# One product moved behind the silu switch, and rows of B spread at unit ends, in the Mamba layer of a four-layer stack

## The chip, the cores and the metric

The kernel runs on one core of one Trainium2 chip. The metric is device time of one launch in microseconds. All names of engines are those of the profile: PE is TensorE, PEld its weight loads, DVE is VectorE, ACT is ScalarE, POOL is GpSimd, SP is the queue that issues DMAs.

## The reference

Four layers work on an image tensor x of 8 images, 192 channels and 56 by 56 positions, each as `x = x + layer(group_norm(x))`. Layer 0 is an involution. Layers 1, 2 and 3 are selective scans (Mamba blocks); layer 1 runs the block three times for each image, on 64 channels each, with an inner width of 512. Cut to what matters here:

```python
xz = x @ in_proj_W.T                       # xi, z
xc = silu(causal_conv4(xi) + conv_b)
dbl = xc @ x_proj_W.T                      # dt_rank | B (16 states) | C (16 states)
dt = softplus(dbl[..., :DT_RANK] @ dt_proj_W.T + dt_proj_b)
h  = h * exp(dt * A) + (dt * xc) * B       # for each position, channel and state
y  = sum_over_states(h * C) + xc * D
y  = y * silu(z)
out = y @ out_proj_W.T
```

## The kernel before

Positions are cut into chunks of 448 (8 rows of the image), 7 chunks to an image, 56 in all. A job is one chunk through one block: layer 1 has 168 jobs (three a chunk, called kinds 0, 1 and 2 here, after the index i in `mamba_jobs`), layers 2 and 3 have 56 each. A job is cut into units: nd groups of 128 channels times NQ = 4 quarters of the states. Layer 1 has nd = 4, so 16 units a job, m = 0 to 15, and 2688 units; layers 2 and 3 have nd = 3, so 12 units a job. One unit holds 4 rows (r) of 448 positions on 128 partitions, where a partition is a channel and a state.

The order of all instructions is written out by hand in `ssm_layer`, unit by unit, and each engine works through its own stream in that order. For unit k the steps are:

- `decays(k, h)` (L749), ACT: exp(dt * A) into the PSUM tiles da0 and da1, two rows for each half h.
- `inputs_begin(k)` (L757), ACT: the carried state goes into column 0 of the tile uhg (nine buffers); issued three units ahead.
- The product (dt * xc) * B into uhg, for half of the units by POOL (`inputs_by_pool`, L768, B from rows in SBUF that SP loads, issued two units ahead), for the others by DVE (`inputs_by_vector`, L774, issued one unit ahead, B from PSUM).
- `spread_b(k)` (L743), PE: for a unit of DVE, one bf16 matmul that spreads the row of B to all 128 partitions, into a pool of one PSUM bank. So the next one can't be written before the product that reads the last one is done.
- `scan(k, 0)` and `scan(k, 1)` (L778), DVE: the recurrence, two scans of 898 positions.
- `keep(k)` (L782), ACT: the last state goes to the carry.
- `readout(k)` (L787), POOL: h * C in place, issued two units late. `reduce(k)`, PE: the sum over the states (L796), with the D term ahead of it for the first quarter of a group (L793), issued three units late.
- `gated(g)` (L812), DVE: times silu(z), at the start of the unit with q = 3. `nothing` (L802): matmuls with a zero weight, as filler on PE.

Beside this the next job is prepared, in steps with costs that `places` deals out over the 32 places of a job (two a unit: before `scan(k, 0)` and before `scan(k, 1)`): convolution (L1046), silu, x_proj (L621), the left-over parts of B (L632, L633), the deltas (L655), softplus (L663), dt times x (L667 on PE, L670 on DVE), the gate (L1064). Two of them are blocks that change ACT's table of functions and change it back. The first is the silu switch: silu of the next job's xc (L616) and of this job's z (L597), ended by a table load (L589). It lies at place 6, so in unit m = 3 of layer 1; the last job's `out_proj` (L1074, L1076, ten matmul passes on PE) follows at place 7 of the same unit. The second is softplus, in unit 7 where the job is of kind 0 and in unit 9 where it is of kind 1 or 2.

In layer 1 POOL has the products of units 1, 3, 5, 7, 9, 11, 13 and 15 before the change, and SP loads rows of B for the quarters 1 and 3. The stream of a unit reads, cut to what the change touches:

```python
scan(k, 0); decays(k + 1, 0); inputs_begin(k + 3)
inputs_by_pool(k + 2); readout(k - 2)
inputs_by_vector(k + 1)
spread_b(k + 2)
bg.run(plan[2 * m + 1]); nothing(k - 3, more > 1)
load_when_free(k)
scan(k, 1); keep(k); decays(k + 1, 1)
```

Of the kernel before, what the change touches and what calls it, by code (L numbers as in the profile page):

```python
# [86 lines left out]
def conv_mamba_stack(ctx: ExitStack, tc: tile.TileContext, a, out):  # L87
# [503 lines left out]
    def with_gates(ops, u):  # L591


        def all_ops():
            ops()
            if u is not None:
                nc.scalar.activation(u.zs, u.zs, AF.Silu)  # L597

        table_block(all_ops)
# [112 lines left out]
    def ssm_layer(pool, w, jobs, n_slots):  # L712


        nd = w.nd
        units = [(i, j, q) for i in range(len(jobs)) for j in range(nd) for q in range(NQ)]
        groups = [(i, j) for i in range(len(jobs)) for j in range(nd)]
        per_job = nd * NQ
        pool_units = {1, 3, 5, 7, 9, 11, 13, 15} if nd == 4 else {1, 3, 6, 7, 9, 11}
        pool_rows = sorted({m % NQ for m in pool_units})  # L720
        us = [Layer() for _ in jobs]
        carry = []
        for s in range(n_slots):
# [1 line left out]
        reps, brow, uhg, ys = {}, {}, {}, {}  # L725

        def load_ops(g):

            i, j = groups[g]
            reps[g] = t = pool.tile([128, NR, 2, T], F32, tag="rep", name="rep", bufs=2)  # L730
            for r in range(NR):
                src = us[i].ops[j][32 * r : 32 * r + 32].rearrange("e c t -> e (c t)")
                nc.sync.dma_start(
                    out=t[:, r].rearrange("p c t -> p (c t)"), in_=src.unsqueeze(1).to_broadcast([32, 4, 2 * T])
                )

        def spread_b(k):

            if k in by_pool:
                return  # L740
            i, j, q = units[k]
            brow[k] = banks.b.tile([128, 512], F32, tag="b", name="b")
            nc.tensor.matmul(brow[k][:, :T], lhsT=pick_b[:, q, :], rhs=us[i].parts, start=True, stop=True)  # L743

        def decays(k, h):
            i, j, q = units[k]
            t = banks.da[h]
            for r in range(2):
                nc.scalar.activation(  # L749
                    t[:, 64 + 449 * r : 512 + 449 * r], reps[k // NQ][:, 2 * h + r, 0, :], AF.Exp, scale=w.neg_a[:, j * NR + 2 * h + r, q : q + 1]  # L750
                )

        def inputs_begin(k):
            i, j, q = units[k]
            uhg[k] = pool.tile([128, NR, T + 1], F32, tag="uhg", name="uhg", bufs=9)
            before = zeros[:, :NR] if jobs[i][1] else carry[jobs[i][0]][:, j, q, :]
            nc.scalar.copy(uhg[k][:, :, 0:1], before.unsqueeze(2))  # L757

        by_pool = {k for k in range(len(units)) if (k % per_job) in pool_units}

        def inputs_by_pool(k):
            if k not in by_pool:
                return
            i, j, q = units[k]
            b = us[i].rows[0, q].unsqueeze(1).to_broadcast([128, NR, T])
            nc.gpsimd.tensor_mul(uhg[k][:, :, 1:], reps[k // NQ][:, :, 1, :], b)  # L768

        def inputs_by_vector(k):  # L770
            if k in by_pool:
                return
            b = brow[k][:, :T].unsqueeze(1).to_broadcast([128, NR, T])
            nc.vector.tensor_mul(uhg[k][:, :, 1:], reps[k // NQ][:, :, 1, :], b)  # L774

        def scan(k, h):
            v = uhg[k][:, 2 * h : 2 * h + 2, :].rearrange("p r t -> p (r t)")
            nc.vector.tensor_tensor_scan(v, banks.da[h][:, 63:961], v, 0.0, ALU.mult, ALU.add)  # L778

        def keep(k):  # L780
            i, j, q = units[k]
            nc.scalar.copy(carry[jobs[i][0]][:, j, q, :].unsqueeze(2), uhg[k][:, :, T:])  # L782
# [6 lines left out]
        def reduce(k):  # L789
            i, j, q = units[k]  # L790
            if q == 0:
                ys[k // NQ] = banks.y.tile([128, 512], F32, tag="y", name="y")
                nc.tensor.matmul(ys[k // NQ][:, :T], lhsT=w.dd[:, j, :], rhs=us[i].xc[:, j, :], start=True, stop=False)  # L793
            y = ys[k // NQ]
            for r in range(NR):
                nc.tensor.matmul(y[32 * r : 32 * r + 32, :T], lhsT=fold, rhs=uhg[k][:, r, 1:], start=False, stop=(q == NQ - 1))  # L796

        def nothing(k, n):

            if k >= 0 and units[k][2] < NQ - 1:  # L800
                for _ in range(n):
                    nc.tensor.matmul(  # L802
                        ys[k // NQ][:, : nd * 112], lhsT=zeros, rhs=w.dd.rearrange("p j e -> p (j e)")[:, : nd * 112],
                        start=False, stop=False,
                    )

        def load_of(steps):
            return sum(st.cost for st in steps if st.matmuls)

        def gated(g):  # L810
            i, j = groups[g]
            nc.vector.tensor_mul(us[i].zs[:, j, :], us[i].zs[:, j, :], ys[g][:, :T])  # L812

        n_places = 2 * per_job
        def bounds(job):

            silu = 8 if nd == 3 else 6
            softplus = silu + (6 if nd == 3 else 8 if job[0] == 1 else 12)
            return (0, silu), (silu, silu + 2), (silu + 2, softplus), (softplus, softplus + 1), (softplus + 2, softplus + 4), (softplus + 4, n_places)

        def places(*stretches):

            plan = [[] for _ in range(n_places)]
            for steps, first, end in stretches:
                todo, debt = list(steps), 0.0
                for p in range(first, end):
                    room, closed = (sum(st.cost for st in todo) + debt) / (end - p) - debt, False
                    while todo and (room > 1e-6 and not closed or p == end - 1):  # L830
                        if (todo[0].block if p % 2 else todo[0].settles) and p < end - 1:
                            break
                        plan[p].append(todo[0])
                        closed = todo[0].closes
                        room -= todo.pop(0).cost
                    debt = max(0.0, -room)
            return plan
# [21 lines left out]
        n_units = len(units)  # L859

        def load_when_free(k):

            g = len(reps)
            if g < len(groups) and k >= NQ * g - NQ - 1 and groups[g][1] in us[groups[g][0]].ops:
                load_ops(g)

        for k, (i, j, q) in enumerate(units):
            m = k % per_job
            if m == 0:

                fetch, outs, rest = tail
                if i + 1 < len(jobs):
                    u = us[i + 1]
                    at = bounds(jobs[i + 1])
                    stretches = *jobs[i + 1][2](u, us[i], outs), rest + jobs[i + 1][3](u)
                    plan = places(*((steps, *p) for steps, p in zip(stretches, at)))
                else:
                    gates = Step(None, lambda: with_gates(lambda: None, us[i]), 0, 0.3, block=True)
                    plan = places(([gates], 4, 6), (outs + rest, 8, n_places))
                plan[3][:0] = [Step(None, fetch, 2, 0.0)]  # L880

            if i + 1 < len(jobs) and m - (per_job - NQ) in pool_rows:
                us[i + 1].row_in(0, m - (per_job - NQ))
            if i and m < NQ:
                us[i].row_in(1, m)
            if k >= NQ + 3 and q == 3:
                gated(k // NQ - 1)
            if k >= 3:
                reduce(k - 3)

            more = 3 - math.ceil(load_of(plan[2 * m] + plan[2 * m + 1]))
            nothing(k - 3, more > 2)
            bg.run(plan[2 * m])
            nothing(k - 3, more > 0)
            load_when_free(k)
            scan(k, 0)
            if k + 1 < n_units:
                decays(k + 1, 0)
            if k + 3 < n_units:
                inputs_begin(k + 3)  # L900
            if k + 2 < n_units:
                inputs_by_pool(k + 2)
            if k >= 2:
                readout(k - 2)
            if k + 1 < n_units:
                inputs_by_vector(k + 1)
            if k + 2 < n_units:
                spread_b(k + 2)
            bg.run(plan[2 * m + 1])
            nothing(k - 3, more > 1)  # L910
            load_when_free(k)
            scan(k, 1)
            keep(k)
            if k + 1 < n_units:
                decays(k + 1, 1)
            if m == per_job - 1:
                tail = jobs[i][4](us[i])
# [333 lines left out]
```

## Time and profile before

| | |
|---|---|
| time, median of 3 runs | 24955.37 us (24948.31 to 24965.5) |
| the profiled execution: time, span | 24963.74 us, 24961.9 us |
| mean granted PE clock | 0.817 |
| layer 1, from its first scan to the first of layer 2 | 1607.75 to 17125.96 us, 15518.21 us |
| layer 2, layer 3 | 3976.24 us, 3859.70 us |
| DVE busy | 22616.8 us (91%) |
| POOL busy | 23597.2 us (95%) |
| PE busy, ACT busy | 21153.9 us (85%), 17043.4 us (68%) |

Time and span are of one execution; the median is of three others. Busy is a share of the span. A row of the groups of instructions gives the line, the engine and the operation, output and inputs by name, shapes and count, then the busy time in us and the mean of one in ns, then the idle time of the engine just before them and what ended it. A row of the timeline gives the start and the length in us, and in square brackets the idle time ahead of it.

### The profile page before, as it was taken

The numbers are of one execution on the slowest core, as the hardware profiler recorded it, in microseconds if no ns is written. First come the engines' busy times: TensorE is split into PE (matmuls) and PEld (weight loads), VectorE is DVE, ScalarE is ACT, GpSimd is POOL, SyncE is SP. The second block draws the span as 40 slices with busy tenths as digits, with TensorE's granted clock in tenths as the row PEclk, the third lists the DMA queues.
The fourth block names the chain that finished last, engine by engine and source line by source line (L and its number), as shares of the span: only waits on it lengthen the run. The fifth ranks groups of instructions, "written<-read, shape, count | busy, mean of one in ns | idle before, by whom it ended". The sixth has DMA issues, their size and how long they took to land.

```text
span 24961.9 us, 237862 instructions
## 1 busy us (share of the span) xinstructions
PE 21153.9 (85%) x74220; PEld 6587.3 (26%) x74220; DVE 22616.8 (91%) x15661; ACT 17043.4 (68%) x32578; POOL 23597.2 (95%) x6996
## 2 busy tenths in 40 slices
PE   8988888888888888888888888888888888888888
PEld 2222222222222222222222222222333332333332
DVE  8989999999999999999999999997999998999998
ACT  2247777777767777777777777776777776777776
POOL 6679999999999999999999999998999998999999
PEclk9987777777777777777777777778888888888888
DMA  4433333333333333333333333333444443444443
GB/s 110 110 108 123 121 123 123 121 121 124 124 122 121 123 123 123 122 123 122 121 125 123 121 122 122 125 122 112 140 132 139 139 138 121 140 141 143 142 141 127
DMA packets 1184899, 3132.97 MB, mean 126 GB/s; under 512 B 163756, under 2 KB 446404, under 8 KB 1183496
## 3 DMA queue, kind: packets, MB, share of 16 engines
q1 hardware_dynamic: 1180824, 3116.70, 38.2%
q8 instruction: 582, 9.54, 0.2%
q14 instruction: 693, 5.68, 0.1%
q10 hardware_dynamic: 2800, 1.06, 0.0%
HBM read 2399.92 MB, written 555.55 MB: 118 GB/s over the span
## 4 chain that ended last, share of the span: by engine, by line
DVE 35%; PE 24%; ACT 17%; issue 11%; POOL 7%; DMA 4%; SPq 1%; DVEq 0%; POOLq 0%; ACTq 0%
DVE uhg L778 24%; ACT da L749 8%; DVE uhg L774 7%; PE y L796 4%; POOL uhg L787 4%; PE mm L655 4%; DMA rows<-bc 2%; PE y L802 2%; POOL uhg L768 2%; ACT L589 2%; PE y L793 2%; PE mm L632 2%; DMA rep<-ops 2%; ACT zs L597 1%; PE mm L429 1%
## 5 line engine op out<-in xcount | busy, mean ns | idle before, releaser
L778 DVE TENSOR_TENSOR_SCAN uhg<-da,uhg 128x898 f32<-128x898 f32 x8064 | 15905.1, 2009 | 1279.9 <-ACT da L749 1276.6
L787 POOL TENSOR_TENSOR uhg<-uhg,rows 128x1792 f32<-128x1792 f32 x4032 | 14739.8, 3676 | 275.4 <-ACT carry L782 267.4
L749 ACT ACTIVATE da<-rep,k 128x448 f32<-128x448 f32 x16128 | 10254.0, 636 | 1669.3 <-DVE uhg L778 1291.5
L768 POOL TENSOR_TENSOR uhg<-rep,rows 128x1792 f32<-128x1792 f32 x2016 | 8038.6, 3987 | 481.6 <-DMA rows<-bc 212.7
L796 PE MATMUL y<-uhg,k 128*32 128x448 f32 x32256 | 4780.6, 669 | 757.6 <-POOL uhg L787 755.3
L774 DVE TENSOR_TENSOR uhg<-rep,b 128x1792 f32<-128x1792 f32 x2016 | 4025.5, 1997 | 468.8 <-PE b L743 424.1
L782 ACT COPY carry<-uhg 128x4 f32<-128x4 f32 x4032 | 787.3, 195 | 3547.9 <-DVE uhg L778 3464.2
L793 PE MATMUL y<-xc,w_d 128*128 128x448 f32 x2016 | 1485.7, 832 | 1390.0 <-DVE zs L812 1388.3
L802 PE MATMUL y<-w_d,k 128*128 128x448 f32 (+1 forms) x5276 | 2496.8, 581 | 0.0
L796 PEld LDWEIGHTS y<-uhg,k 128*32 128x32 f32 x32256 | 695.9, 117 | 3858.8 <-issue 2203.8
L655 PE MATMUL mm<-dbl,w_dt 36*128 36x448 f32 (+1 forms) x2016 | 1501.2, 858 | 155.0 <-ACT k L637 155.0
L1102 PE MATMUL mm<-v,w_in 96*128 96x448 f32 x2688 | 1464.8, 677 | 170.1 <-ACT zs L694 71.1
L802 PEld LDWEIGHTS y<-w_d,k 128*128 128x128 f32 x5276 | 1050.9, 214 | 1480.4 <-issue 1452.5
L1046 PE MATMUL mm<-xs,k 128*128 128x448 f32 x2688 | 1229.7, 592 | 112.4 <-ACT zs L694 100.5
L1129 PE MATMUL mm<-xin,w_conv 128*128 128x448 f32 x2688 | 1077.9, 543 | 1.0 <-ACT xin L696 0.9
L441 DVE TENSOR_TENSOR prod<-mm,shifted 128x448 f32<-128x448 f32 x1680 | 928.6, 611 | 141.2 <-PE mm L429 63.5
L632 PE MATMUL mm<-dbl,k 16*16 16x448 f32 x1120 | 687.8, 702 | 422.7 <-ACT dbl L625 422.7
L667 PE MATMUL mm<-xc,k 128*128 128x448 f32 x2016 | 971.4, 592 | 30.8 <-DVE dt L670 29.7
L793 PEld LDWEIGHTS y<-xc,w_d 128*128 128x128 f32 x2016 | 443.3, 258 | 2056.5 <-DVE zs L812 1392.8
L1064 PE MATMUL mm<-xs,k 64*128 64x448 f32 x1344 | 861.6, 750 | 109.0 <-ACT zs L694 109.0
L743 PE MATMUL b<-k,k 96*128 96x448 bf16 x2016 | 832.2, 413 | 126.8 <-DVE uhg L774 126.6
L449 POOL TENSOR_TENSOR x<-x,one 96x448 f32<-96x448 f32 x560 | 631.1, 1134 | 265.9 <-DVE one L441 248.4
(138 smaller groups left out, 19672.2 us busy)
## 6 DMA issues: line engine op xcount, KB each, us to landing
rep<-ops SPq DMA_DIRECT2D x4032, 448.0 KB, 5.9
ops<-dt SPq DMA_DIRECT2D x1008, 448.0 KB, 3.3
rows<-bc SPq DMA_DIRECT2D x1792, 224.0 KB, 6.2
shifted<-xpad SPq DMA_DIRECT2D x672, 179.0 KB, 4.5
xg<-stream SPq DMA_DIRECT2D x168, 336.0 KB, 3.8
xr<-stream SPq DMA_DIRECT2D x168, 336.0 KB, 5.3
stream<-xr SPq DMA_DIRECT2D x112, 336.0 KB, 3.4
xs<-xg SPq DMA_DIRECT2D x224, 112.0 KB, 2.3
```

The costliest lines, as they stand in the source:

```text
L632: nc.tensor.matmul(u.left[m][:NS, :T], lhsT=ident[:NS, :NS], rhs=u.dbl[:NS, :], start=True, stop=False)
L655: nc.tensor.matmul(u.dps[j][:, :T], lhsT=w.dtw[:, j * 128 : (j + 1) * 128], rhs=u.dbl[:nk, :], start=True, stop=True)
L749: nc.scalar.activation(t[:, 64 + 449 * r : 512 + 449 * r], reps[k // NQ][:, 2 * h + r, 0, :], AF.Exp, scale=w.neg_a[:, j * NR + 2 * h + r, ...
L768: nc.gpsimd.tensor_mul(uhg[k][:, :, 1:], reps[k // NQ][:, :, 1, :], b)
L774: nc.vector.tensor_mul(uhg[k][:, :, 1:], reps[k // NQ][:, :, 1, :], b)
L778: nc.vector.tensor_tensor_scan(v, banks.da[h][:, 63:961], v, 0.0, ALU.mult, ALU.add)
L787: nc.gpsimd.tensor_mul(v, v, us[i].rows[1, q].unsqueeze(1).to_broadcast([128, NR, T]))
L793: nc.tensor.matmul(ys[k // NQ][:, :T], lhsT=w.dd[:, j, :], rhs=us[i].xc[:, j, :], start=True, stop=False)
L796: nc.tensor.matmul(y[32 * r : 32 * r + 32, :T], lhsT=fold, rhs=uhg[k][:, r, 1:], start=False, stop=(q == NQ - 1))
L802: nc.tensor.matmul(ys[k // NQ][:, : nd * 112], lhsT=zeros, rhs=w.dd.rearrange("p j e -> p (j e)")[:, : nd * 112], start=False, stop=False,)
L1046: nc.tensor.matmul(pm[:, :T], lhsT=w.inconv[:, k, j * 128 : (j + 1) * 128], rhs=ck.xs[:, i, 2 - 2 * k : 2 - 2 * k + T], start=(k == 0), st ...
L1102: nc.tensor.matmul(pm[:, :T], lhsT=w.inw[:, k, m * 128 : (m + 1) * 128], rhs=ck.v[:, k, :], start=(k == 0), stop=(k == NCT - 1),)
```

## The change

In layer 1, except in the last job, unit 5 goes from POOL to DVE and unit 6 from DVE to POOL. Unit 5's product is issued on DVE at the end of unit 3, after `scan(k, 1)`, so two units ahead, not one; it is skipped where its old place comes up. POOL's product for unit 6 is issued in unit 4, where that for unit 5 was issued in unit 3. So POOL and DVE keep eight products a job each. As unit 6 is a third quarter, SP loads a third row of B for each job of layer 1.

In layer 1 the rows of B are no longer spread in the middle of the unit, two units ahead of their own, but at the end of a unit, behind its filler and ahead of `scan(k, 1)`, as soon as the last spread row has been read by a product issued in this unit or before: after the products of units 0, 2, 4, 5, 8, 10, 12 and 14. In layers 2 and 3 the order stays as it was.

```diff
-        pool_units = {1, 3, 5, 7, 9, 11, 13, 15} if nd == 4 else {1, 3, 6, 7, 9, 11}
-        pool_rows = sorted({m % NQ for m in pool_units})
+        def pool_units(i):
+            if nd == 3:
+                return {1, 3, 6, 7, 9, 11}
+            return {1, 3, 5 if i + 1 == len(jobs) else 6, 7, 9, 11, 13, 15}
+        pool_rows = (1, 2, 3)
...
         def spread_b(k):
-            if k in by_pool:
+            if k in by_pool or k in brow:
                 return
...
+        def spread_next_b(done):
+            n = len(brow)
+            if n < len(by_vector) and by_vector[n - 1] <= done:
+                spread_b(by_vector[n])
...
-        by_pool = {k for k in range(len(units)) if (k % per_job) in pool_units}
+        by_pool = {i * per_job + m for i in range(len(jobs)) for m in pool_units(i)}
+        by_vector = [k for k in range(len(units)) if k not in by_pool]
+        multiplied = set()
...
         def inputs_by_vector(k):
-            if k in by_pool:
+            if k in by_pool or k in multiplied:
                 return
+            multiplied.add(k)
...
                 inputs_by_vector(k + 1)
-            if k + 2 < n_units:
+            if nd == 3 and k + 2 < n_units:
                 spread_b(k + 2)
             bg.run(plan[2 * m + 1])
             nothing(k - 3, more > 1)
+            if nd == 4:
+                spread_next_b(k + 1)
             load_when_free(k)
             scan(k, 1)
+            if i + 1 < len(jobs) and m == at[1][0] // 2 and k + 2 not in by_pool:
+                inputs_by_vector(k + 2)
             keep(k)
```

## The prediction

> **What bounds the kernel now.** I read first the busy time of each engine over layer 1 alone, since layers 2 and 3 keep their order.
>
> ```profile
> core 0: us, PE busy (x) PEld busy (x) DVE busy (x) ACT busy (x) POOL busy (x), PEclk, DMA share, GB/s
> 1607.75:17125.96 15518.21, 13002.81 (x40251) 3757.20 (x40251) 14143.72 (x8597) 10980.48 (x20999) 15071.59 (x4048) 0.77 0.36 122
> ```
>
> DVE is idle for 15518 − 14144 = 1374 us, POOL for 447. No change in order alone that keeps POOL's work can gain more than 447 us. Second, the waits of layer 1, longest first, for who idles for whom (total, times, longest):
>
> ```profile
> DVE uhg L778 <- ACT da L749: 742.3, 394, 3.8
> DVE uhg L774 <- PE b L743: 369.0, 222, 2.7
> ACT k L637 <- PE mm L633: 372.0, 167, 3.1
> ```
>
> No scan waits for POOL: layer 1 runs at DVE's pace, and DVE stalls behind ACT (742) and for rows of B (369). Third, the timeline, with every idle stretch of DVE put to its kind and unit. The same 2.84 us stand in unit 3 of each job, 477 in all: the silu switch. The waits for b are 0.7 a job in unit 1 of kind 1, 1.2 in unit 7 of kind 0, 2.6 and 2.0 in unit 9 of kinds 1 and 2. Waits for da at 1.3 stand in unit 8 of kinds 1 and 2. Here is unit 3 of a job of kind 1, then one of kind 2, DVE before PE in each:
>
> ```profile
> 7217.71 2.02 DVE L778 TENSOR_TENSOR_SCAN uhg<-da,uhg 128x898 f32<-128x898 f32 x1
> 7219.65 1.99 DVE L774 TENSOR_TENSOR uhg<-rep,b 128x1792 f32<-128x1792 f32 x1
> 7221.56 2.02 DVE L778 TENSOR_TENSOR_SCAN uhg<-da,uhg 128x898 f32<-128x898 f32 x1
> 7226.42 5.86 DVE L778 TENSOR_TENSOR_SCAN uhg<-da,uhg 128x898 f32<-128x898 f32 x3 [2.85 <-ACT da L749]
> ...
> 7217.85 1.02 PE L793 MATMUL y<-xc,w_d 128*128 128x448 f32 x2 [1.61 <-DVE zs L812]
> ...
> 7221.77 5.32 PE L1076 MATMUL mm<-zs,w_out 128*64 128x448 f32 x8
> ```
>
> ```profile
> 7318.22 5.86 DVE L778 TENSOR_TENSOR_SCAN uhg<-da,uhg 128x898 f32<-128x898 f32 x3 [2.85 <-ACT da L749]
> ...
> 7309.65 1.02 PE L793 MATMUL y<-xc,w_d 128*128 128x448 f32 x2 [3.10 <-DVE zs L812]
> ...
> 7312.38 3.22 PE L1076 MATMUL mm<-zs,w_out 128*64 128x448 f32 x8
> ```
>
> The reader is to see two things. DVE waits 2.85 us behind the switch, room for one product of 1.99. And PE works all this time: `out_proj` ends at 7227.09, after the waiting scan's start at 7226.42, in the first job; at 7315.60, 2.6 before it, in the second. The granted clock over the 8.71 us was 0.61 in the first and 1.00 in the second. Over 162 jobs `out_proj` ends late (9 us or more after the unit's first scan) in 0 of 54 of kind 0 (6 lie between), 49 of 54 of kind 1 and 23 of 54 of kind 2.
>
> **The product in the stall.** DVE keeps its number of products. The one it loses, unit 6's, shortens unit 5 from 5.77 to 3.84 us, so by 1.93; the one it gains costs what doesn't fit in the stall. Its row of B is the catch. In the changed program's PE stream this spread stands behind `out_proj`, as both belong to the second half of unit 3.
> - `out_proj` at full clock: ends 7315.60, spread 0.36 (the short L743 rows), product from 7316.0 to 7318.0. The scan started at 7318.22, so nothing is lost: −1.93.
> - `out_proj` at half clock: ends 7227.09, spread 0.4, product from 7227.5 to 7229.5. The scan started at 7226.42: +3.07, less 1.93 is +1.14. Queued behind the waiting product on DVE are all scans from unit 4 on; for those wait ACT's decays and, behind these in ACT's queue, the copy of dbl (L625) on which the next job's deltas hang.
>
> **What the deltas make of it.** In unit 5 PE begins the chain to the next softplus when ACT has copied dbl (L625), behind unit 6's first decays:
>
> ```profile
> 7136.21 0.92 PE L632 MATMUL mm<-dbl,k 16*16 16x448 f32 x2 [2.63 <-ACT dbl L625]
> ...
> 7147.37 0.56 PE L743 MATMUL b<-k,k 96*128 96x448 bf16 x1
> ```
>
> Between these rows of a kind 0 job PE has no idle time at all, at a clock of 0.54. A DVE that is 1.93 earlier in unit 6 does not make this chain earlier. In kind 0 the last delta goes to ACT at 7147.48, softplus and its two table loads end at 7153.72, and unit 8's first scan waits for the decay behind them: the 1.93 is waited off there, so I put kind 0 at 0, with its 1.2 for b too (the same wait lies behind it). In kind 2 the like chain ends in unit 8's wait for da; only a spread of 0.5 leaves it (unit 8's row, now spread at the end of unit 4, where PE waits for dbl anyhow), so I put −0.5. In kind 1 with a late `out_proj`, PE waits 1.7 for ACT inside the chain, which takes the 1.14, so DVE's +1.14 stays as it is.
>
> **The rows at unit ends.** The next spread comes half a unit to one and a half units sooner. In unit 9 of a kind 1 job DVE waited until 7256.12 for b, 2.67 us. Without that the unit's second scan ends at 57.4, but the next two instructions are L670, which read PE's L667, and PE, without the spread, ends those at about 58.5 and 59.4 (58.05 + 1.77 with it). So the next unit's first scan starts at 59.95, not 61.04: −1.1, and the same for kind 2. Unit 1 of kind 1: −0.7, as nothing waits behind it. What it adds: PE, in order, stands at the spread until this unit's product is done, and the reduces behind it stand too. Sorted by unit, PE now comes to the end of the units 1, 3, 4, 7 and 15 later than that product (by 0.9 to 6.5 us), so it doesn't stand; in unit 9 of kind 0 and unit 13 of kind 1 it comes 4.7 and 3.5 early and will stand, ahead of a reduce whose reader is over a unit away. Cost nothing; if that cover is gone, up to 3 us in one job of three.
>
> **POOL and the queues.** POOL's product moves behind one more readout; POOL runs about two units ahead of the scans with its products, so unit 6's is in time. In kind 1 the readout that follows loses its filler and waits about 1.9 for the carry, inside 5.3 us that POOL idles in that job. SP's third row adds 168 loads of 224 KB (6.2 us from issue to landing), behind the row for unit 1 and ahead of that for unit 3. POOL now idles 75 us in layer 1 for such rows; I bound the cost by 0 and another 75 and take 0, since the row that is waited for goes first.
>
> **Sum for a chunk**, with the clocks as they are: kind 0 about +0.1 (the six between), kind 1 +1.14 − 1.1 − 0.7 = −0.7, kind 2 31/54 × (−1.6) + 23/54 × 0 = −0.9. Together −1.5, times 56 is −85 us, against the execution's 24963.74. The median of the runs is 8 us lower, so 24870.
>
> [...]
>
> **Rivals.**
> - PE late in most jobs. For it: kind 1 is late already, kind 2 in 23 of 54, and the clock follows small shifts in time. Against: kind 0 was never fully late. The price is 3.07 in kind 0, where it goes down the softplus chain whole: 3.07 − 0.7 + 0 = +2.4 a chunk, +134 us, 25090. If also the gains at b fail, 3.07 + 1.14 + 1.14 = +5.35, +300. It decides from about every second job of kind 0 late.
> - PE early in most jobs: kind 1 becomes −1.93 − 1.1 − 0.7 = −3.7, kind 2 −1.6: −5.3 a chunk, −297 us, 24660. This leaves POOL 150 of its 447 idle us. Against it is kind 1 today.
> - The stall only moves: what is won at b is waited off behind the chain of deltas as in kind 0, and early and late jobs cancel: 24955.
>
> **How the numbers follow.** Mixed clocks 0.45 (own range 24790 to 24950), PE late 0.28, PE early 0.17, no net change 0.10. A difference of 0.2%, 50 us, is about what a measurement of this kernel can tell. Of the first case I count 0.32 as faster, 0.09 within, the rest slower: faster 0.50, same 0.17, slower 0.33. The range leaves out the ends of both large rivals: 24690 to 25080.
>
> **What would show it.** DVE's idle time in unit 3 falls from 2.84 to about 0.9 where `out_proj` is early, and a wait of the new product for b of 3 us or more stands there where it is late. Unit 5 takes 3.9 us. The 369 us for b fall to about the late jobs' share, and the waits for da in units 7 and 8 grow. If those do not grow, the chain of deltas is no bound and the gain is larger; if unit 3's scan in kind 0 starts 3 us later, I am wrong to the slow side.

## The result, and the profile after

The changed kernel takes 25107.65 us (median of 4 runs), the one before 24957.25 beside it: a ratio of 1.0058, 95% interval 1.0043 to 1.0073. It is slower by 150 us. That is above the range, and within 20 us of the price of the rival in which PE is late (25090), to which I had given a chance of 0.28.

The busy times over layer 1 of the changed kernel, from the first scan to the first of layer 2:

```profile
1615.48:17255.44 15639.96, 13277.55 (x40247) 3844.34 (x40247) 14198.90 (x8598) 10952.67 (x20999) 15079.22 (x4048) 0.76 0.36 123
```

Layer 1 is 122 us longer (15518 before), with DVE idle for 1441 us, not 1374. The other 29 us of the profiled execution lie in layers whose order is the same: 11 and 10 in layers 2 and 3, 8 ahead of layer 1. Differences of this size stand between the traces of this study (layer 0 took 1576 to 1622 us in them by the same code), so they are not put down to the change. DVE's waits in layer 1, total, times, longest:

```profile
DVE uhg L793 <- ACT da L761: 495.1, 380, 3.8
DVE uhg L789 <- PE b L749: 292.4, 166, 4.8
```

The wait for decays has fallen by 247 us: the product does fill the switch's stall. The wait for rows of B has not gone: it was 369 us in 222 places, and is 292 in 166, nearly one for each job. Sorted by unit these all stand in unit 3. Here is unit 3 of a job of kind 0, DVE, then PE:

```profile
7171.16 2.02 DVE L793 TENSOR_TENSOR_SCAN uhg<-da,uhg 128x898 f32<-128x898 f32 x1
7176.99 2.02 DVE L789 TENSOR_TENSOR uhg<-rep,b 128x1792 f32<-128x1792 f32 x1 [3.81 <-PE b L749]
7178.93 5.86 DVE L793 TENSOR_TENSOR_SCAN uhg<-da,uhg 128x898 f32<-128x898 f32 x3
...
7167.45 1.02 PE L808 MATMUL y<-xc,w_d 128*128 128x448 f32 x2 [2.56 <-DVE zs L827]
...
7171.73 4.92 PE L1095 MATMUL mm<-zs,w_out 128*64 128x448 f32 x8
7176.59 0.36 PE L749 MATMUL b<-k,k 96*128 96x448 bf16 x1
```

`out_proj` (L1095) takes 4.92 us, not the 3.22 that it took at a clock of 1.00, unit 5's row (L749) comes behind it, and DVE waits 3.81 us for that. The scan of unit 4 starts 11.62 us after that of unit 3, not 8.71. The stretch between these two scans, in the same job before the change and after it (the columns are as in the prediction's first view, the third from the end is the granted clock):

```profile
7121.61:7130.32 8.71, 7.96 (x31) 2.18 (x32) 5.87 (x5) 8.59 (x12) 8.71 (x3) 1.00 0.60 207
7167.31:7178.93 11.62, 11.48 (x33) 2.90 (x34) 7.81 (x6) 10.40 (x15) 11.62 (x5) 0.71 0.48 158
```

The trace sorted by kind of job tells where this happens. Late means, as in the prediction, that `out_proj` ends 9 us or more after the first scan of unit 3.

| layer 1 | kind 0 | kind 1 | kind 2 |
|---|---|---|---|
| us a job, before | 95.0 | 92.5 | 87.8 |
| us a job, after | 98.6 | 91.7 | 87.1 |
| late of 54 jobs, before | 0 | 49 | 23 |
| late of 54 jobs, after | 49 | 7 | 0 |
| granted clock in unit 3, before | 0.98 | 0.64 | 0.83 |
| granted clock in unit 3, after | 0.73 | 0.94 | 1.00 |

A chunk (three jobs) went from 275.3 to 277.5 us. In unit 3 the half clock has moved from kinds 1 and 2 to kind 0.

### The profile page after: what moved, and what is told of

Same layout as the page of the kernel before. It is cut to its first block, busy times and chain, and to the rows that moved or that the text cites. A ratio compares the mean times of both kernels' runs of the same rounds, so it can differ in the third digit from the quotient of the medians.

```text
span 25112.4 us, 238377 instructions
## 1 busy us (share of the span) xinstructions
PE 21466.8 (85%) x74220; PEld 6678.7 (27%) x74220; DVE 22675.7 (90%) x15661; ACT 17015.6 (68%) x32578; POOL 23604.7 (94%) x6996
## 4 chain that ended last, share of the span: by engine, by line
PE 35%; DVE 30%; ACT 12%; issue 11%; POOL 6%; DMA 4%; SPq 1%; DVEq 0%; POOLq 0%; ACTq 0%
DVE uhg L793 21%; PE y L811 7%; DVE uhg L789 5%; ACT da L761 5%; PE mm L655 5%; POOL uhg L802 4%; DMA rows<-bc 3%; PE y L817 3%; PE y L808 3%; PE mm L632 3%; PE mm L667 3%; PE mm L1095 2%; POOL uhg L782 2%; PE mm L1065 2%; PE mm L429 1%
## 5 line engine op out<-in xcount | busy, mean ns | idle before, releaser
L811 PE MATMUL y<-uhg,k 128*32 128x448 f32 x32256 | 4922.5, 687 | 599.6 <-POOL uhg L802 598.1
L808 PE MATMUL y<-xc,w_d 128*128 128x448 f32 x2016 | 1540.3, 860 | 1363.1 <-DVE zs L827 1362.3
L632 PE MATMUL mm<-dbl,k 16*16 16x448 f32 x1120 | 764.3, 774 | 637.7 <-ACT dbl L625 637.7
L1065 PE MATMUL mm<-xs,k 128*128 128x448 f32 x2688 | 1171.5, 573 | 62.3 <-ACT zs L694 40.2
L749 PE MATMUL b<-k,k 96*128 96x448 bf16 x2016 | 822.9, 408 | 352.6 <-DVE uhg L789 352.3
L670 DVE TENSOR_TENSOR dt<-dt,mm 128x448 f32<-128x448 f32 x1008 | 611.9, 614 | 416.2 <-PE mm L667 120.8
```

What stands on the lines that cost most here:

```text
L632: nc.tensor.matmul(u.left[m][:NS, :T], lhsT=ident[:NS, :NS], rhs=u.dbl[:NS, :], start=True, stop=False)
L1065: nc.tensor.matmul(pm[:, :T], lhsT=w.inconv[:, k, j * 128 : (j + 1) * 128], rhs=ck.xs[:, i, 2 - 2 * k : 2 - 2 * k + T], start=(k == 0), st ...
```

## The experiments

Theory 1: the loss is unit 5's row, which stands behind an `out_proj` at half clock. Theory 2: the rows at unit ends make PE stand for DVE's products, and so late in all it does. The first four kernels tell these apart. All four ratios are against 24957 us.

**Rows at unit ends alone.** The edit to the changed kernel:

```diff
-            return {1, 3, 5 if i + 1 == len(jobs) else 6, 7, 9, 11, 13, 15}
+            return {1, 3, 5, 7, 9, 11, 13, 15}
...
-        pool_rows = (1, 2, 3)
+        pool_rows = (1, 3) if nd == 4 else (1, 2, 3)
...
-            if i + 1 < len(jobs) and m == at[1][0] // 2 and k + 2 not in by_pool:
-                inputs_by_vector(k + 2)
```

> Rows of B at unit ends as in the changed kernel, but units 1, 3, 5, ... stay with POOL, no early product, two rows of B from SP. Theory 1 (the loss is the row of unit 5 standing behind a slow out_proj in kind 0): no wait for b in unit 3, the waits for b in units 1 and 9 go, part of that is given back behind the chain of deltas: 24850 to 24950. Theory 2 (the loss comes from PE standing at spreads at the unit ends, which makes PE late): about 25060 to 25110, nearly all of the loss.

24901 us, 0.9979 (0.9970 to 0.9988). Theory 2 falls: this half of the change gains 56 us. In no unit of layer 1 is a wait for b left that comes to 0.05 us a job. And the lateness is as after the whole change: `out_proj` is late in 50 of 54 jobs of kind 0 and in none of the others. So it is the rows at unit ends that move it, and by the table above the half clock with it, to kind 0, where without the early product nothing waits for it (kind 0 takes 94.6 us).

**The product alone**, with rows in the middle of the unit as before:

```diff
-            if nd == 3 and k + 2 < n_units:
+            if k + 2 < n_units:
                 spread_b(k + 2)
...
-            if nd == 4:
-                spread_next_b(k + 1)
```

> The early product and the exchange of units 5 and 6, but rows of B in the middle of the unit, two ahead, as before; unit 5's row is then spread ahead of out_proj. Theory 1: no wait of unit 5's product for b beyond 0.5 us, unit 5 at 3.9 us, the 369 us of other waits for b stay; out_proj stands until unit 4's product is done (about 2 us), so the chain of deltas starts later: 24880 to 25000. Theory 2: the whole saving of the early product shows, 24700 to 24850.

24872 us, 0.9965 (0.9953 to 0.9976), between the ranges, 8 us under that of theory 1 and 22 over that of theory 2. Each half of the change gains, 56 and 86 us; together they lose 150. With the row ahead of `out_proj` no wait for b is left in unit 3, though `out_proj` itself now ends late in all jobs of kinds 1 and 2.

**Unit 5's row ahead of `out_proj`**, the rest as in the changed kernel:

```diff
+            if nd == 4 and i + 1 < len(jobs) and m == at[1][0] // 2:
+                spread_next_b(k + 1)
             bg.run(plan[2 * m + 1])
```

> The changed kernel, with unit 5's row alone spread ahead of out_proj in unit 3, all other rows at unit ends. Theory 1: the wait for b in unit 3 goes in all kinds, kind 0 falls by 2 to 3.5 us a job: 24880 to 24980. Theory 2: as the changed kernel, 25080 to 25130, since PE now stands one spread earlier.

24710 us, 0.9902 (0.9886 to 0.9919): 397 us under the changed kernel, and far under what I expected. One matmul's place decides the sign.

**The row inside `out_proj`**, after its third of five steps:

```diff
+            banks.halfway = (lambda k=k: spread_next_b(k + 1)) if nd == 4 and m == 3 else None
             bg.run(plan[2 * m + 1])
...
+                            if j == 1 and banks.halfway:
+                                banks.halfway()
```

> The changed kernel, with unit 5's row spread in the middle of out_proj, after its third of five steps, so that PE neither stands for unit 4's product nor keeps DVE waiting, at half clock either. Theory 1: no wait for b in unit 3 over 0.5 us, the fastest of these: 24800 to 24920. Theory 2: as the changed kernel, 25080 to 25130.

24832 us, 0.9950 (0.9935 to 0.9965). Theory 1 again, but not the fastest, and with 2.2 us of wait for b left in unit 3 of kind 0 and 1.0 in that of kind 1: there even three steps of `out_proj` end too late.

The kernel with the row first gained more than the wait for b is worth. In the changed kernel PE idles through unit 5 of kinds 1 and 2 (busy for 0.02 and 0.08 of it) and then works at a clock of 0.50 in units 6 to 8; with the row first it does not idle (0.94 and 0.96). Unit 5 and then units 6 to 8 of a job of kind 2 of the changed kernel:

```profile
7369.88:7373.72 3.84, 0.32 (x1) 0.00 (x0) 3.84 (x3) 3.14 (x8) 3.84 (x2) 0.93 0.00 0
7373.72:7390.28 16.56, 16.46 (x37) 4.01 (x41) 14.13 (x10) 11.42 (x26) 16.56 (x5) 0.50 0.35 114
```

PE is busy for 0.32 of 3.84 us, then for all of the next 16.56 at a clock of 0.50, and DVE waits for the decays behind it in unit 8:

```profile
7388.33 3.94 DVE L793 TENSOR_TENSOR_SCAN uhg<-da,uhg 128x898 f32<-128x898 f32 x2 [2.42 <-ACT da L761]
```

The half clock in units 6 to 8 is not new, though. Here is the same job before the change, unit 5 and units 6 to 8:

```profile
7322.09:7327.85 5.76, 1.83 (x3) 0.25 (x3) 5.76 (x4) 3.61 (x8) 5.76 (x3) 0.75 0.04 11
7327.85:7343.26 15.41, 15.41 (x36) 3.59 (x38) 14.08 (x9) 10.97 (x24) 15.41 (x5) 0.50 0.35 119
```

The next three kernels keep the changed kernel's order (the third that with the row first) and put fillers, matmuls with a zero weight that nobody waits for, where PE idles. The ratios are against 24981 us, the kernel before beside them; as that is 24 us more than beside the changed kernel, a difference from the changed kernel given below can be off by so much.

**Fillers ahead of unit 3 in kind 0:**

```diff
+            if nd == 4 and m == 2 and k > 4 and jobs[i][0] == 0:
+                nothing(k - 4, 2)
             if k >= 3:
                 reduce(k - 3)
```

> The changed kernel with two filler matmuls (zero weight) at the start of unit 2 in jobs of kind 0 alone, where PE otherwise idles 2.6 us ahead of unit 3. Nothing of DVE's order changes. Theory 1 (the granted clock makes kind 0's out_proj late): the clock in unit 3 of kind 0 goes from 0.73 to about 1.0, out_proj ends early in most of these 54 jobs, and kind 0 falls from 98.6 us to about 95: 24880 to 24950. Rival (the lateness is PE's work ahead of out_proj, so more work makes it later): 25110 or more.

25051 us, 1.0031 (1.0021 to 1.0041). Neither: 56 us faster than the change (67 by the ratios), not 160 to 230. The trace says why. These are the stretches of unit 3 in a job of kind 0 and the next of kind 1, and the latter's product:

```profile
7137.67:7146.38 8.71, 8.57 (x33) 2.40 (x34) 7.89 (x5) 8.59 (x12) 8.71 (x4) 1.00 0.61 204
7232.95:7244.60 11.65, 11.52 (x32) 2.94 (x33) 7.80 (x5) 10.39 (x15) 11.65 (x4) 0.71 0.48 159
```

```profile
7242.66 2.02 DVE L789 TENSOR_TENSOR uhg<-rep,b 128x1792 f32<-128x1792 f32 x1 [3.85 <-PE b L749]
```

In kind 0 more work ahead made `out_proj` earlier: 8.71 us at full clock, late in 0 of 54 jobs, 96.1 us a job, not 98.6. But now kind 1 is late in 48 of 54, and takes 93.6, not 91.7. The half clock went to the next job.

**Fillers at the end of unit 4:**

```diff
                 spread_next_b(k + 1)
+                if m == 4:
+                    nothing(k - 3, 3)
```

> The changed kernel with three filler matmuls at the end of unit 4 of each job of layer 1, where PE in kinds 1 and 2 idles through unit 5 until dbl is copied (busy 0.02 and 0.08). Theory of the clock: the idle unit 5 is what halves the clock in units 6 to 8 (0.50 now); with it filled the clock there rises, the wait for da in unit 8 (2.4 us in kinds 1 and 2) falls under 1 us, and the kernel gains 1.5 to 2 us in two jobs of three: 24890 to 24960, kind 0 aside. Rival (the chain of deltas is long by its work, not by its clock): more work on PE, 25100 to 25200.

24831 us, 0.9942 (0.9926 to 0.9959): 277 us under the changed kernel, more than expected, by more work. The same job of kind 2, unit 5 and units 6 to 8:

```profile
7267.95:7271.78 3.83, 2.21 (x11) 0.46 (x10) 3.83 (x3) 3.14 (x8) 3.83 (x3) 1.00 0.00 0
7271.78:7286.25 14.47, 13.79 (x42) 3.46 (x43) 14.09 (x9) 11.34 (x26) 14.47 (x5) 0.70 0.39 131
```

The clock after it is 0.70, not 0.50, the stretch takes 14.47 us, not 16.56, and unit 8's wait falls from 2.4 to 0.7 and 0.5 us in kinds 1 and 2. Kind 2 goes from 87.1 to 84.4 us. The wait for b in unit 3 stays (353 us in all). Not all of the 277 us is the clock behind unit 5: `out_proj` is now late in 21 jobs of kind 0 and 33 of kind 1, and kinds 0, 1 and 2 gain 0.9, 1.2 and 2.7 us a job.

**Both cures:** the same fillers in the kernel with unit 5's row first.

```diff
+            if nd == 4 and i + 1 < len(jobs) and m == at[1][0] // 2:
+                spread_next_b(k + 1)
             bg.run(plan[2 * m + 1])
...
                 spread_next_b(k + 1)
+                if m == 4:
+                    nothing(k - 3, 3)
```

> The kernel with unit 5's row ahead of out_proj (24710) with the same three fillers at the end of unit 4. There PE is busy through unit 5 already (0.94 to 0.96) and the clock in unit 6 is 0.93 to 0.97 in kinds 1 and 2. Theory of the clock: nothing left to gain, and the fillers lie in the chain: 24720 to 24850. Rival (fillers cost nothing and help anyhow): under 24700.

24712 us, 0.9898 (0.9881 to 0.9915): the same as without the fillers, 24710, and 8 us under the first range. The clock in units 7 and 8 of kind 1 went from 0.64 and 0.53 to 1.00 and 0.99, and a chunk takes 270.5 us in both kernels: with the row first this chain at half clock no longer sets the time.

Two more kernels ask whether the clock explains all of it, and whether it was to be had without the change. The ratios are against 24971 us.

**Fillers in the kernel before**, two at the end of unit 4:

```diff
             nothing(k - 3, more > 1)
+            if nd == 4 and m == 4:
+                nothing(k - 3, 2)
             load_when_free(k)
```

> The kernel before, with two filler matmuls at the end of unit 4 of each job of layer 1 and nothing else. If the half clock in units 6 to 8, and not the amount of work, holds the chain of deltas also there, the waits for da in unit 8 of kinds 1 and 2 (1.3 us) and for b in unit 9 (2.6 and 2.0) shrink by more than half: 24750 to 24880. Rival (the fillers only lengthen PE's queue): 24950 to 25050.

24937 us, 0.9989 (0.9980 to 0.9998): between the two ranges, a gain of 0.1%. In unit 6 the clock rose (0.67 to 0.86 in kind 1, 0.51 to 0.70 in kind 2), but the waits in units 8 and 9 hardly moved (1.3 to 1.2; 2.6 and 2.0 to 2.4 and 1.8). Units 7 and 8 stay near 0.5 there.

**Both fillers in the changed kernel**, the three of unit 4 as above and the two of unit 2, now in kinds 0 and 1:

```diff
+            if nd == 4 and m == 2 and k > 4 and jobs[i][0] < 2:
+                nothing(k - 4, 2)
```

> The changed kernel with the fillers of unit 4 and those of unit 2 (two, now in kinds 0 and 1). If out_proj is early in all three kinds and the clock stays up in units 6 to 8, both losses of the change go: 24650 to 24750, as fast as the kernel with unit 5's row first. If the half clock only moves to another kind, as it did with the fillers of unit 2 alone, the wait for b in unit 3 stays in one kind: 24780 to 24860.

24713 us, 0.9901 (0.9885 to 0.9918): 395 us less than the changed kernel, with its order of all but fillers as it was. `out_proj` is late in no job of any kind (40 of kind 0 lie between early and late), and the waits in layer 1 are:

```profile
DVE uhg L793 <- ACT da L761: 338.8, 445, 3.2
DVE uhg L789 <- PE b L749: 130.8, 166, 1.6
```

## Why the prediction was wrong

**The step that failed first is the sum "with the clocks as they are".** It took the share of late jobs by kind from the trace of before (0, 49 and 23 of 54) and priced the change in each kind. The change made it 49, 7 and 0. Fewer jobs are late in all, 56 for 72, but they are now where lateness costs most. I had written that the clock follows small shifts in time, as a point for the rival, and then gave the unchanged mix the largest chance. The rows at unit ends alone show the move; the fillers in unit 2 show that it moves again by two matmuls, and what it is worth: late against early is 98.6 to 96.1 us in kind 0 and 93.6 to 91.7 in kind 1, by the means of a kind in the two kernels. The sign that I had named for the slow side is what came: the scan behind the switch in kind 0 starts 2.9 us later in a late job.

By kind the sum had +0.1, −0.7 and −0.9 us a job; measured are +3.6, −0.8 and −0.7. So kind 0 is the whole miss, and that the other two agree is luck: they were priced as late or partly late, and came early, mostly, without the gain that early jobs were to have. The nearness of the rival's 25090 to the result is luck in part, too, as it had all three kinds late. (The chances of faster, same and slower add up to 0.49, 0.19 and 0.32 by the cases given, not 0.50, 0.17 and 0.33.)

**The price of a late job was right in its mechanism.** Worked out: a wait of 3.07 past the old start of the scan, in kind 0 down the chain of deltas whole. Measured: kind 0 went from 95.0 to 98.6, +3.6 (by the means of its units +2.6 in unit 3, −1.9 in unit 5, +2.5 in unit 6, where the decays and the gate wait for PE, and +0.4 elsewhere). So the 1.9 is waited off, as forecast, but 1.0 us of the 3.6 is not lateness: with the fillers of unit 2 kind 0 is early and still takes 96.1 us, with unit 6 at 7.6 us, not 4.7. The sum had an early kind 0 at nothing; why unit 6 loses more than unit 5 gains stays open.

**The second step that failed is the gain of early jobs.** The sum for all early was −3.7 in kind 1 and −1.6 in kind 2; in the run kind 1 was early in 41 of 54 jobs, which take 91.2 us (−1.4), and kind 2 in all (−0.7). The early product is there (unit 5 takes 3.84 us, as forecast), and so are the gains at b (unit 1 −0.8, unit 9 −1.6 and −0.9). But in kind 1 unit 8's wait for decays grew from 1.3 to 2.4 us, unit 10 is 0.6 longer, and the wait for the next chunk's norm (L563 in unit 11) went from 1.5 to 2.8. From the first scan of unit 3 to that of unit 9 an early job of kind 1 takes 33.0 us, 33.7 before: more than half of the 1.93 is waited off there. I had let this chain of deltas bind in kinds 0 and 2 and let it go in kind 1.

In kind 2 the same stretch is 1.1 us shorter, more than the 0.5 of the sum. What the sum lacks in kind 2 is unit 10, 0.6 longer, and unit 2, 1.0 longer, where the gate waits for PE, at a clock of 0.50 and 0.76 in units 0 and 1 (0.98 and 0.99 before):

```profile
7080.65 0.62 DVE L827 TENSOR_TENSOR zs<-zs,y 128x448 f32<-128x448 f32 x1 [0.87 <-PE y L811]
```

I also had the chain's length fixed. From the first L632 to the last delta it took 16.5 us in kinds 1 and 2 before, and takes 15.8 after, at mean clocks of 0.60 and 0.53 before and 0.50 after. The fillers at the end of unit 4 make it 12.8 and 12.3 and shorten unit 8's wait by 1.7 and 1.9 us. In the kernel before, where PE was busy for 0.79 and 0.54 of unit 5, they do nothing of the kind (15.9 and 16.1). So an idle unit 5 is not the only thing that goes before the half clock; what holds it at 0.5 in units 7 and 8 there stays open.

**What held.** With `out_proj` early the product fits: in unit 3 of kind 2 a wait of 0.55 us for b is all that stands. Kind 0 gains nothing even where DVE waits for no row in unit 3: 95.0 us with the product alone (95.0 before). That PE's standing at the unit ends costs nothing is not shown: with these rows alone all 369 us of waits for b are gone, but layer 1 is only 77 us shorter, and L563 waits 3.0 us in unit 11 of kind 1, not 1.5. POOL's waits for rows from DMA in layer 1 went from 75 to 111 us, inside the bound of 75 more, of which I had taken none; the kernel with the rows at unit ends, but without the third load, has 107, so the load itself is hardly in it.

**What the traces show of the clock.** In the clock records of the trace of before the granted clock is 1.00 or 0.50, and its 1582 stretches are, but for the last, whole multiples of 3.413 us. Ahead of the 791 falls in that trace PE was busy for 0.40 of the last 3.413 us (the median). And fillers in idle stretches raised the clock of the work behind: with those of unit 2, where 2.56 us lay idle ahead of unit 3 of kind 0, from 0.71 to 1.00; with those of unit 4, where 3.62 us lay idle in unit 5 of kind 2, from 0.50 to 0.70. But the half clock also held where PE was not idle: in units 6 to 8 of the job of kind 2 above PE is busy for 15.41 of 15.41 us before the change and for 16.46 of 16.56 after it, more than four times 3.413 us each, and the clock stays at 0.50.

Nor does the length of the gap ahead of unit 3 tell the clock there: 2.56 us in the job of kind 0 stood before a clock of 0.71, where in the same job before the change 3.10 stood before full clock. Before the change gaps over 3 us stood there in 21, 25 and 52 jobs of the three kinds, of which 0, 25 and 23 were late; of the 29 of kind 1 with a shorter gap 24 were late too. What sets the clock is not shown by these runs.

## What to carry to other kernels

Before an instruction is moved into a stall, look at what stands ahead of its inputs in the other engines' queues, and at the slowest clock that this work has had anywhere in the trace: one matmul behind ten made the difference between −247 and +150 us. A share of jobs at half clock is not a constant that a sum may take from the trace of before; price all jobs late and all early, and ask which order does not depend on it. And where PE idles ahead of a chain that others wait for, a few matmuls of zeros can make the chain shorter (15.8 to 12.3 us here); whether they do has to be tried, as in the kernel before they did not.

## What was not expected of the hardware

Three different kernels end at the same length of layer 1, to 1.1 us in 15255: unit 5's row first, that with fillers, and the change with both fillers.

```profile
1589.13:16844.16 15255.03, 12752.09 (x40247) 3729.33 (x40247) 14187.39 (x8598) 10943.10 (x20999) 15065.81 (x4048) 0.79 0.37 126
```

```profile
1615.01:16870.47 15255.46, 13070.78 (x41699) 3947.38 (x41699) 14191.05 (x8597) 10943.15 (x20999) 15065.66 (x4048) 0.81 0.37 126
```

Their clocks differ (0.79 and 0.81, and 0.82 for the third), POOL's busy time does not: it idles for 186 to 190 us of the span, 107 of these (in the first) in two waits at the end of the layer. So POOL's work looks like the floor of layer 1 under this split of the products: the 447 us that I named as the most that could be gained are used up but for 189, though no run took work from POOL to prove it. Of the three, which are equally fast, unit 5's row ahead of `out_proj` is the one that needs no filler: 24710 us, 1.0% under the kernel before.
